# Two transformer layers on one core: the first norm of layer 1 transposed by DMA in two 16-bit planes

## The chip, the core and the metric

The kernel runs on one core of a Trainium2 chip. A core has a matrix engine (TensorE, PE in the profile, with its weight loads as PEld), a vector engine (VectorE, DVE), an engine for activation functions (ScalarE, ACT), a general engine (GpSimd, POOL), and SyncE (SP), which here issues DMAs only. They run side by side, each through its own list of instructions in order, and wait for one another through semaphores. The metric is the device time of one execution in microseconds (us); lower is better.

## What is computed

Inputs x (2 x 2048 tokens, 512 features) and a context of 2 x 128 tokens go through two layers. Each layer is an attention from x to the context and a feed-forward part, each with a layer norm in front and a residual sum behind:

```
x = x + L0_xattn(norm(x), context)      16 heads of 64, rotary positions, tanh cap
x = x + L0_ffn(norm(x))                 fake-quantised gate, up and down projections, 1408 wide
x = x + L1_xattn(norm(x), context)      16 heads of 32, with biases and a mask
x = x + L1_ffn(norm(x))                 a gate of 512 logits; the token's argmax modulo 8
                                        picks one of 8 experts (512 x 512)
norm(x) = (x - mean(x)) / sqrt(var(x) + 1e-5)
```

The change concerns the third line: the norm in front of layer 1's attention and the way its result reaches the query projection, Q = norm(x) Wq^T + bq. A matrix product on TensorE sums over the partitions, so the normed tile, whose partitions are tokens, has to be turned until its partitions are features.

## The kernel before

The 4096 tokens are 32 tiles of 128 tokens, one token per partition, and stay on the chip from end to end (`xs[n]`, 128 x 512 fp32). The kernel has four stretches: layer 0's attention (to about 680 us), the gate and up projections (to about 845 us), the down projection merged with the start of layer 1 (to about 950 us), and layer 1's attention merged with the gate of the experts and then the experts themselves (to the end).

The order of work is written out by hand. From the down projection on, TensorE, VectorE, ScalarE and GpSimd execute their instructions in exactly the order in which the program states them. Only SyncE's list, the DMAs, is put in order by the scheduler, and it too is then executed in order.

*The down projection* (loop at the end of the program, `for n in range(NT - held)`): for each tile n, `rounded(n + 2)` loads 704 KB of hidden values from memory and ScalarE rounds them to 8 bits (L798), `widened(n + 1)` makes bf16 of them on VectorE (L803), `down(n)` runs 11 matmuls on TensorE (L809), VectorE scales the result into `y` (two buffers, L811) and GpSimd adds it to x (L812). Near its end the first two pairs of tiles of layer 1 are prepared: their norms at n = 22 and 26, their turning (`turned1`) after the `down` of n = 23 and 27. In between, `queries` of block 0 run.

*The loop over tiles* (`for n in range(NT)`) has one tile per iteration and two tiles per block (`B1 = 256` tokens). The steps of iteration n that matter here, in program order:

- `biased(n - 1)`: GpSimd adds the output bias to the residual (L926).
- `rest1 = normed(...)`: the statistics of tile n + 4, which is tile t of block blk + 2: bn_stats on VectorE, then the power -1/2 on GpSimd (L100).
- `scores(n)`: 16 products of queries and keys on TensorE (L869), mask and maxima on VectorE.
- `queries(blk + 1, ...)`: half of this tile's share of the next block's query projection (L849), which reads `xT` of block blk + 1; ScalarE adds the bias (L852).
- `exponentials(n)` on ScalarE (L891); `shares(n, 0)`, `shares(n, 1)`: sums on VectorE, the products on GpSimd (L900); `logits(n - 2)` on TensorE (L955) between them.
- `rest1()`: VectorE centres and scales tile n + 4 into `xn1` (L820).
- `projected(n - 1)`, `normed2(n - 1)()`: the output projection (L932), then the second norm of that tile, again with a power on GpSimd and a centring on VectorE.
- the other half of `queries`; additions to the expert weights on GpSimd for tiles 4 to 19 (L1230); `turned(n)`: the shares transposed on TensorE and copied by ScalarE (L908); the store of a finished row tile to memory (L982); `turned2(n - 1)`: the second norm transposed, with a ScalarE copy (L949); `mixed(n)`: shares times values on TensorE (L918), copied by ScalarE to `oT` (L923).
- at the end of the block's second tile, `turned1` for both tiles of block blk + 2: four 128 x 128 transposes per tile on TensorE (L115) into PSUM, and a ScalarE copy into `xT` (L840). `xT` has one buffer; the next iteration's `queries` is its first reader, straight after `scores`.

During iterations 0 to 2 the eight expert weights of 1 MB each are loaded by SyncE.

Of the kernel before, what the change touches and what calls it, by code (L numbers as in the profile page):

```python
# [13 lines left out]
I32 = mybir.dt.int32  # L14
U32 = mybir.dt.uint32
U8 = mybir.dt.uint8
I8 = mybir.dt.int8
AF = mybir.ActivationFunctionType
ALU = mybir.AluOpType
# [4 lines left out]
P = 128  # L24
B, S, T, D = 2, 2048, 128, 512
ND = D // P
NT = B * S // P
# [31 lines left out]
NB1 = B1 // P  # L59
# [3 lines left out]
def two_layers(ctx: ExitStack, tc: tile.TileContext, a, out):  # L63
    nc = tc.nc
# [8 lines left out]
    def load(dst, src):  # L73
        nc.sync.dma_start(out=dst, in_=src)
# [36 lines left out]
    def transposed(psum, src, n=ND):  # L111

        pt = psum.tile([P, n, P], F32, name="pt", tag="m")
        for c in range(n):
            nc.tensor.transpose(pt[:, c, :], src[:, c * P : (c + 1) * P], ident)  # L115
        return pt
# [33 lines left out]
    with ExitStack() as l0:  # L150
        w0 = l0.enter_context(tc.tile_pool(name="w0", bufs=1))
        psm = l0.enter_context(tc.tile_pool(name="psm", bufs=2, space=PSUM))
# [13 lines left out]
        mid = l0.enter_context(tc.tile_pool(name="mid", bufs=2))  # L166
# [5 lines left out]
        cosk, sink = (xs[homes[22]][:, i * T : (i + 1) * T] for i in range(2))  # L172
        padu = w0.tile([P, B], U8, name="padu")
        for b in range(B):
# [152 lines left out]
        def normed(k):  # L327


            stats[k] = small.tile([P, NB0, 2], F32, name="stat")  # L330
            for t, n in enumerate(tiles[k]):
                mv = variance(xs[n])
                ve = small.tile([P, 1], F32, name="ve")
                nc.vector.tensor_scalar(ve, mv[:, 1:2], 1.0 + EPS, EPS * EPS, ALU.mult, ALU.add)
                nc.vector.tensor_copy(stats[k][:, t, 0:1], mv[:, 0:1])
                nc.gpsimd.tensor_tensor(stats[k][:, t, 1:2], ve, minus_half, ALU.pow)
            if k > 1:
                features_in(k)
                turned_in(k)
# [247 lines left out]
    bob = wa.tile([P, D], F32, name="bob")  # L587
    masks = wa.tile([P, TPB, T], U8, name="masks")
    ones1 = wa.tile([P, DH1], F32, name="ones1")


    def table(shape, pattern, base=0, channel=0, dtype=BF16):
# [17 lines left out]
        out=before, in_=before, pattern=[[1, P]], compare_op=ALU.is_ge, fill=0.0, base=-1, channel_multiplier=-1  # L610
# [25 lines left out]
    with ExitStack() as up:  # L636
        psm = up.enter_context(tc.tile_pool(name="psm_ff", bufs=2, space=PSUM))
# [99 lines left out]
        for blk in range(NT // NBF):  # L737
            for i in range(NI):
                pg = psg.tile([P, BF], F32, name="pg")
                pu = psg.tile([P, BF], F32, name="pu")  # L740
                for w, dst in ((wgT, pg), (wuT, pu)):
# [7 lines left out]
                h = work.tile([P, NBF, P], F32, name="h", bufs=4)  # L749
# [5 lines left out]
                    out=h_dram[blk * NBF : (blk + 1) * NBF, :, i, :].rearrange("t p q -> p t q"), in_=h  # L755
                )

                t, odd = divmod(i, 2)
                n = (blk + 1) * NBF + t
# [3 lines left out]
                if i >= 3 and i % 2 == 1:  # L763
                    n = (blk + 1) * NBF + (i - 3) // 2
# [9 lines left out]
        rest = values(0)  # L774
        sh, ish = act_step(psm, "L0_ffn_clip_down", hmax)
        rest()
        rest = values(1)
# [5 lines left out]
    psm = l1.enter_context(tc.tile_pool(name="psm_l1", bufs=4, space=PSUM))  # L783
    pss = l1.enter_context(tc.tile_pool(name="pss_l1", bufs=1, space=PSUM))
    big = at.enter_context(tc.tile_pool(name="big1", bufs=1))
    mid = at.enter_context(tc.tile_pool(name="mid1", bufs=2))
# [28 lines left out]
    scs, xTs, qTs, keeps, ss_, sums, pTs_, os_ = {}, {}, {}, {}, {}, {}, {}, {}  # L815
    xn1s = {}

    def center_by(dst, x, mean, r):

        nc.vector.scalar_tensor_tensor(dst, x, mean, r.to_broadcast([P, D]), ALU.subtract, ALU.mult)  # L820

    def normed(n):

        mv = variance(xs[n])
        r = small.tile([P, 1], F32, name="r")
        rsqrt_eps(r, mv[:, 1:2])

        def rest():
            xn1s[n] = mid.tile([P, D], F32, name="xn1")
            center_by(xn1s[n], xs[n], mv[:, 0:1], r)  # L830

        return rest

    def turned1(n):

        blk, t = divmod(n, NB1)
        if t == 0:
            xTs[blk] = big.tile([P, ND, B1], F32, name="xT1")
        pt = transposed(psm, xn1s[n])
        nc.scalar.copy(xTs[blk][:, :, t * P : (t + 1) * P], pt)  # L840

    def queries(blk, fs):

# [93 lines left out]
    def normed2(n):  # L937

        mv = variance(xs[n])
        nc.vector.tensor_copy(xw[n][:, D : D + 1], mv[:, 0:1])  # L940
        r = xw[n][:, D + 1 : D + 2]
        rsqrt_eps(r, mv[:, 1:2])
        xn2[n] = mid.tile([P, D], F32, name="xn2", bufs=1)
        return lambda: center_by(xn2[n], xs[n], mv[:, 0:1], r)
# [19 lines left out]
    def gated(n):  # L964

        negm, i8 = picks[n]
        pe = small.tile([P, 1], F32, name="pe1")

        nc.scalar.activation(
            scs[min(n + 2, NT - 1)][:, 0].rearrange("p c k -> p (c k)"), pls[n], AF.Exp, bias=negm, accum_out=pe  # L970
        )
        ei = small.tile([P, 1], U32, name="ei")
        nc.vector.tensor_scalar(ei, i8[:, 0:1], NE - 1, None, ALU.bitwise_and)
        ef = small.tile([P, 1], F32, name="ef")
        nc.vector.tensor_copy(ef, ei)
        nc.vector.tensor_scalar(hot[:, n, :], iota_e, ef, None, ALU.is_equal)
        nc.gpsimd.tensor_tensor(cum[:, n + 1, :], cum[:, n, :], hot[:, n, :], ALU.add)
        nc.vector.memset(xw[n][:, D + 3 : D + 4], 0.0)

        def rest():  # L980
            nc.vector.reciprocal(xw[n][:, D + 2 : D + 3], pe)
            nc.sync.dma_start(out=x_dram[n * P : (n + 1) * P, :], in_=xw[n])  # L982

        return rest
# [173 lines left out]
    held = 4  # L1158
    widened(0)
    rounded(1)  # L1160
    rests = []
    for n in range(NT - held):
        rounded(n + 2)
        widened(n + 1)
        for rest in rests:
            rest()
        down(n)
        rests = []
        if n == NT - held - 6:
            rests = [normed(t) for t in range(NB1)]  # L1170
        if n == NT - held - 5:
            for t in range(NB1):
                turned1(t)
        if n >= NT - held - 4:
            f = n - NT + held + 4
            queries(0, range(f, f + 1))
        if n == NT - held - 2:
            rests = [normed(NB1 + t) for t in range(NB1)]
        if n == NT - held - 1:
            for t in range(NB1):  # L1180
                turned1(NB1 + t)
# [5 lines left out]
    for n in range(NT):  # L1187
        blk, t = n // NB1, n % NB1
        ahead = blk + 1 < nblk
        fs = range(t * ND // NB1, (t + 1) * ND // NB1)  # L1190
        if n > 0:
            biased(n - 1)
        rest1 = normed((blk + 2) * NB1 + t) if blk + 2 < nblk else None
        scores(n)
        if ahead:
            queries(blk + 1, fs[:1])
        exponentials(n)
        if n == 0:
            for i in range(NT - held, NT - held + 2):
                down(i)  # L1200
                widened(i + 2)
        shares(n, 0)
        if n > 1:
            logits(n - 2)
        shares(n, 1)
        if rest1:
            rest1()
        if n > 0:
            projected(n - 1)
            normed2(n - 1)()  # L1210
        rest = gated(n - 2) if n > 1 else None
        if n + 1 < NT:
            kept_keys(n + 1)
        if ahead:
            queries(blk + 1, fs[1:])
        if n == 0:
            for i in range(NT - held + 2, NT):
                down(i)
            dwn.close()
            ffd.close()  # L1220
            moe = ctx.enter_context(tc.tile_pool(name="moe", bufs=1, side="right"))
            we = moe.tile([P, NE, ND, D], F32, name="we")
            for e in range(NE):
                load(we[:, e], a["L1_ffn_We"][e].rearrange("(c p) f -> p c f", p=P))
        if 4 <= n < 4 + 2 * NE:
            e, half = divmod(n - 4, 2)
            if half == 0:
                load(rowadd, v_dram[e].partition_broadcast(P))
            for c in range(2 * half, 2 * half + 2):
                nc.gpsimd.tensor_tensor(we[:, e, c, :], we[:, e, c, :], rowadd, ALU.add)  # L1230
        if not ahead:

            expert(n - NT + NB1)
        turned(n)
        if rest:
            rest()
        if n > 0:
            turned2(n - 1)
        mixed(n)
        if t == NB1 - 1 and blk + 2 < nblk:  # L1240
            for t in range(NB1):
                turned1((blk + 2) * NB1 + t)
        if n == NTA + 2:
            route = routing(True)
        if route:
            for _ in range(3 if n == NTA + 2 else 2):
                if next(route, route) is route:
                    route = None
                    for j in range(4):
                        gathered(j)  # L1250
                    break
        if n == NT - NB1 - 1:
            for j in range(2):
                centered_x(j)
            turned_x2(0)
# [57 lines left out]
```

## Time and profile before

| | us |
|---|---|
| median of 3 runs | 1624.31 (1623.14 to 1624.88) |
| the profiled execution's own time | 1623.87 |
| its span, first to last instruction | 1622.2 |
| TensorE busy | 1566.2 (97%) |
| VectorE busy | 1160.9 (72%) |
| ScalarE busy | 694.1 (43%) |
| GpSimd busy | 583.6 (36%) |
| copies of `turned1` on ScalarE (L840), 32 | 17.3, 0.589 each |
| centring of `xn1` (L820), 32 | 26.1, 0.821 each |

How to read it: a group line gives line, engine, operation, what is written from what, the shape and how often; then the busy time in total and the mean of one in ns; then how long the engine was idle just before these instructions, and what ended that. A timeline line gives the start, the length, and then the same names; a bracket at its end tells an idle time and its releaser. SPq is SyncE's queue: its times are those of issuing a DMA, not of moving the data. PEclk is the share of its clock that TensorE was granted. In the steady part of the loop, from about 975 us, two iterations take 31.8 us.

### The profile page before, as it was taken

Reading aid. Unit: us, or ns where it says so; the run is one execution under the profiler, and the core shown is the slowest. Engines: PE = TensorE matmul, PEld = TensorE weight load, DVE = VectorE, ACT = ScalarE, POOL = GpSimd, SP = SyncE. Lnnn points to the kernel's source line nnn. Section 1 sums busy time; section 2 is a strip of 40 time slices with the busy share of each in tenths; the row PEclk is TensorE's granted clock in tenths of the full one; section 3 lists DMA queues with packets and bytes.
Section 4 is the critical chain, followed back from the end, with each engine's and each line's share of the span. In section 5 each row is a group of like instructions: output and inputs, shape, how many; then the busy total and the mean of one; then the engine's idle time right before and its main releaser. Section 6 shows DMA issues by size and latency. Waiting matters only on the chain. (4 is left out here: it accounts for less than half of the span.)

```text
span 1622.2 us, 26285 instructions
## 1 busy us (share of the span) xinstructions
PE 1566.2 (97%) x9690; PEld 922.2 (57%) x9714; DVE 1160.9 (72%) x2276; ACT 694.1 (43%) x1537; POOL 583.6 (36%) x576
## 2 busy tenths in 40 slices
PE   7999999999999999999999989999999998999997
PEld 5655555655555565434444556666666665654443
DVE  3467777777777875689986678787787879766322
ACT  1222222222222222234336567676766765753332
POOL 2232222222222221110006644555656443544553
PEclk9999999999999999999999999999999999999999
DMA  9511112111111310567659650000000000113332
GB/s 323 178 37 40 46 41 55 40 46 40 47 46 36 77 37 5 160 174 189 180 168 314 221 202 20 28 21 34 27 21 27 14 21 14 40 47 108 128 121 68
DMA packets 135164, 139.64 MB, mean 86 GB/s; under 512 B 51681, under 2 KB 99257, under 8 KB 135036
## 3 DMA queue, kind: packets, MB, share of 16 engines
q1 hardware_dynamic: 125932, 118.07, 23.9%
q0 software_dynamic: 6240, 18.70, 3.6%
q8 instruction: 78, 1.28, 0.3%
q10 hardware_dynamic: 2864, 1.19, 0.3%
q14 instruction: 50, 0.41, 0.1%
HBM read 89.97 MB, written 41.79 MB: 81 GB/s over the span
## 5 line engine op out<-in xcount | busy, mean ns | idle before, releaser
L392 PE MATMUL pq<-xnT,wq 128*128 128x256 f32 x1024 | 254.4, 391 | 0.0
L418 ACT ACTIVATE pr<-sc 128x1024 f32<-128x1024 f32 x64 | 65.6, 1025 | 421.6 <-PE sc L413 421.5
L450 PE MATMUL pw<-wo,att 128*128 128x512 f32 x512 | 230.8, 593 | 0.0
L392 PEld LDWEIGHTS pq<-xnT,wq 128*128 128x128 f32 x1024 | 184.4, 189 | 67.1 <-issue 44.0
L900 POOL TENSOR_TENSOR s<-s,rs 128x1024 f32<-128x1024 f32 x64 | 132.6, 2085 | 185.1 <-DVE rs L899 184.7
L891 ACT ACTIVATE s<-s,mx 128x128 f32<-128x128 f32 x512 | 175.3, 388 | 20.8 <-DVE mx L882 20.8
L402 POOL TENSOR_TENSOR q<-rt,rt 128x256 f32<-128x256 f32 x64 | 46.8, 731 | 339.8 <-DVE rt L401 335.4
L450 PEld LDWEIGHTS pw<-wo,att 128*128 128x128 f32 x512 | 96.9, 190 | 96.4 <-issue 89.9
L440 DVE RECIPROCAL rd<-sc 128x256 f32<-128x256 f32 x64 | 112.4, 1757 | 46.6 <-PE sc L434 46.4
L1146 PE MATMUL pz<-we,x 128*128 x312 | 140.7, 594 | 0.7 <-issue 0.6
L849 PE MATMUL pq<-xT,wq 128*128 128x256 f32 x512 | 124.1, 385 | 0.1
L877 DVE SCALAR_TENSOR_TENSOR s<-sc,keep 128x1024 f32<-128x1024 f32 x64 | 78.0, 1219 | 53.5 <-PE sc L869 45.4
L932 PE MATMUL pw<-wo,oT 128*128 128x512 f32 x256 | 115.2, 592 | 0.7 <-ACT oT L923 0.7
L955 PE MATMUL pl<-wgate,xnT 128*128 128x512 f32 x256 | 115.3, 593 | 0.0
L849 PEld LDWEIGHTS pq<-xT,wq 128*128 128x128 f32 x512 | 94.8, 190 | 28.1 <-issue 13.9
L748 ACT ACTIVATE gate<-pg,gsc 128x512 f32<-128x512 f32 x88 | 60.5, 687 | 96.6 <-PE pg L743 81.4
L397 DVE TENSOR_TENSOR rt<-pq,rope_cos 128x256 f32<-128x256 f32 x64 | 27.0, 422 | 104.3 <-PE pq L392 104.3
L743 PE MATMUL pu<-xqT,wuT 128*128 128x512 bf16 x345 | 90.4, 382 | 4.2 <-DVE h L751 3.8
L91 DVE BATCH_NORM_STATS2 st<-x 128x6 f32<-128x512 f32 x130 | 89.4, 688 | 5.7 <-DMA x<-in_ctx 3.5
L1150 DVE TENSOR_TENSOR x<-x,x 128x512 f32<-128x512 f32 x39 | 27.0, 693 | 90.0 <-ACT x L1149 89.8
L743 PE MATMUL pg<-xqT,wgT 128*128 128x512 bf16 x344 | 90.1, 382 | 0.4
L1146 PEld LDWEIGHTS pz<-we,x 128*128 128x128 f32 x312 | 56.3, 190 | 58.3 <-issue 58.0
(216 smaller groups left out, 2791.9 us busy)
## 6 DMA issues: line engine op xcount, KB each, us to landing
h_dram<-h SPq DMA_DIRECT2D x88, 256.0 KB
hq<-h_dram SPq DMA_DIRECT2D x31, 704.0 KB
x_dram<-x SPq DMA_DIRECT2D x32, 258.0 KB
x<-in_x SPq DMA_DIRECT2D x32, 256.0 KB
we<-in_L_ffn_We SPq DMA_DIRECT2D x8, 1024.0 KB
xnT<-in_x_turned SPq DMA_DIRECT2D x14, 512.0 KB
along<-stat_dram SPq DMA_DIRECT2D x14, 256.0 KB
w_in<-in_L_ffn_w_gate SPq DMA_DIRECT2D x11, 256.0 KB
```

The lines of the kernel that those rows point to most:

```text
L91: nc.vector.bn_stats(out=st, in_=x)
L392: nc.tensor.matmul(pq, wqs[c // 2][:, c % 2, par, g * P : (g + 1) * P], xnTs[k][:, c, :], start=(c == 0), stop=(c == ND - 1))
L440: nc.vector.reciprocal(rd, sc[:, 0, B0:])
L450: nc.tensor.matmul(pw, atts[u][:, f, t * P : (t + 1) * P], wo[:, 2 * g + f, :], start=(g == 0 and f == 0), stop=(g == NG - 1 and f == 1),)
L743: nc.tensor.matmul(dst, w[:, c, i * P : (i + 1) * P], xqTs[blk][:, c, :], start=(c == 0), stop=(c == ND - 1),)
L849: nc.tensor.matmul(pq, wq1[:, c, f * P : (f + 1) * P], xTs[blk][:, c, :], start=(c == 0), stop=(c == ND - 1))
L877: nc.vector.scalar_tensor_tensor(s, sc[:, 2 * half : 2 * half + 2].rearrange("p r c k -> p (r c) k"), -MASKED, keeps[n].unsqueeze(1).to_br ...
L891: nc.scalar.activation(s[:, h, :], s[:, h, :], AF.Exp, bias=mx[:, h : h + 1], **accum)
L900: nc.gpsimd.tensor_tensor(s, s, rs.unsqueeze(2).to_broadcast([P, 8, T]), ALU.mult)
L932: nc.tensor.matmul(pw, os_[n][:, c, :], wo1[:, c, :], start=(c == 0), stop=(c == ND - 1))
L955: nc.tensor.matmul(pl, xn2T[n][:, c, :], wgate[:, c, :], start=(c == 0), stop=(c == ND - 1))
L1146: nc.tensor.matmul(pz, ring[j][:, c, :], we[:, bass.ds(e, 1), c, :], start=(c == 0), stop=(c == ND - 1))
```

## The change

`turned1` no longer uses TensorE. The centred tile `xn1` (128 tokens x 512 fp32) is regarded as 1024 numbers of 16 bits. GpSimd copies them into a tile `planes`, all 512 low halves first and then all 512 high halves (`split`). A transposing DMA, issued by SyncE, turns the eight blocks of 128 x 128 16-bit numbers and writes them back into `xn1`. ScalarE then copies the two planes into `xT` so that the halves of each fp32 lie side by side again (`joined`): 1024 16-bit elements per partition, read in a row and written at steps of four bytes.

In the loop over tiles, `split` stands after `projected(n - 1)` and `normed2(n - 1)`; `joined` stands where the ScalarE copy was. In the down projection `split` follows the centring directly, and the norms of the first two pairs are moved earlier: from n = 22 to 19 and from n = 26 to 23. The turning of both pairs stays where it was.

```diff
+    def split(x):
+        planes = mid.tile([P, 2 * D], U16, name="planes")
+        nc.gpsimd.tensor_copy(
+            planes.rearrange("p (h f) -> p h f", h=2), x.bitcast(U16).rearrange("p (f h) -> p h f", h=2)
+        )
+        nc.sync.dma_start(
+            out=x.bitcast(U16).rearrange("p (b q) -> p b q", q=P), in_=planes, transpose=True
+        )
+
+    def joined(dst, x):
+        nc.scalar.copy(
+            dst.bitcast(U16).rearrange("p c (q h) -> p h c q", h=2),
+            x.bitcast(U16).rearrange("p (h c q) -> p h c q", h=2, c=ND),
+        )
...
             center_by(xn1s[n], xs[n], mv[:, 0:1], r)
+            return lambda: split(xn1s[n])
...
-        pt = transposed(psm, xn1s[n])
-        nc.scalar.copy(xTs[blk][:, :, t * P : (t + 1) * P], pt)
+        joined(xTs[blk][:, :, t * P : (t + 1) * P], xn1s[n])
...
         for rest in rests:
-            rest()
+            rest()()
         down(n)
         rests = []
-        if n == NT - held - 6:
+        if n == NT - held - 9:
             rests = [normed(t) for t in range(NB1)]
         if n == NT - held - 5:
             for t in range(NB1):
                 turned1(t)
+            rests = [normed(NB1 + t) for t in range(NB1)]
...
-        if n == NT - held - 2:
-            rests = [normed(NB1 + t) for t in range(NB1)]
...
         if rest1:
-            rest1()
+            rest1 = rest1()
         if n > 0:
             projected(n - 1)
             normed2(n - 1)()
+        if rest1:
+            rest1()
```

More of the change, by code (lines that the diff above doesn't have):

```diff
@@ L16 @@
 U8 = mybir.dt.uint8
+U16 = mybir.dt.uint16
 I8 = mybir.dt.int8
```

## The prediction

> **What bounds the kernel now.** I read the busy shares first, then the stretch in which the changed step runs, then that stretch's timeline instruction by instruction.
>
> ```profile
> PE 1566.2 (97%) x9690; PEld 922.2 (57%) x9714; DVE 1160.9 (72%) x2276; ACT 694.1 (43%) x1537; POOL 583.6 (36%) x576
> ```
> ```profile
> 975.00:1300.00 325.00, 317.84 (x2432) 213.81 (x2431) 257.75 (x555) 226.25 (x724) 178.07 (x155) 1.00 0.07 23
> ```
>
> In the window table (columns: length, then busy time of PE, PEld, DVE, ACT, POOL, then clock, DMA share, GB/s) TensorE is busy for 318 of 325 us while ScalarE and GpSimd have slack. So taking TensorE work away pays, if nothing that TensorE then waits for comes later than the work taken away. The timeline at the end of an odd tile decides that:
>
> ```profile
> 1124.22 0.55 POOL L100 TENSOR_TENSOR x<-ve,minus_half 128x1 f32<-128x1 f32 x1
> ...
> 1126.26 1.08 PE L918 MATMUL po<-s,v 128*32 128x128 f32 x32
> ...
> 1127.27 1.09 PE L115 MATMUL pt<-ident,xn 128*128 128x128 f32 x8
> 1127.43 0.59 ACT L923 COPY oT<-po 128x512 f32<-128x512 f32 x1 [0.38 <-PE po L918]
> 1127.96 1.07 ACT L840 COPY xT<-pt 128x512 f32<-128x512 f32 x2
> ...
> 1128.29 1.17 PE L869 MATMUL sc<-kT,qT 32*128 32x128 f32 x32
> ...
> 1129.40 1.99 PE L849 MATMUL pq<-xT,wq 128*128 128x256 f32 x8
> ```
>
> The eight transposes occupy TensorE from 1127.27 to 1128.29: 1.02 us. The scores take to 1129.40, and then the next queries read xT, whose two copies ended at 1129.03, 0.37 us early. This is a relay with little room: whatever makes xT ready later than about 1128.4 (1129.40 less the 1.02 saved) stops TensorE, since its order is fixed.
>
> **The change part by part.** Sixteen groups of eight transposes go: two before the loop over tiles, fourteen in it (ends of tiles 1, 3, ... 27). TensorE's order is otherwise as before, so the change does take that work away.
>
> *A block of the loop.* In GpSimd's program order the new copy stands behind the small power instruction shown above (it ends at 1124.77), and its input, the centred tile, is ready since 1122.3. Its price C is not in the trace; nearest rows:
>
> ```profile
> L900 POOL TENSOR_TENSOR s<-s,rs 128x1024 f32<-128x1024 f32 x64 | 132.6, 2085 | 185.1 <-DVE rs L899 184.7
> L349 POOL TENSOR_TENSOR xnT<-xnT,along 128x1024 f32<-128x1024 f32 x14 | 34.9, 2493 | 0.0
> L422 POOL TENSOR_SCALAR_AFFINE_SELECT pr<-pr 128x512 f32<-128x512 f32 x8 | 5.1, 638 | 17.6 <-issue 15.4 <-ACT pr L420 1.5 <-POOL rstd L100 0.7
> L418 ACT ACTIVATE pr<-sc 128x1024 f32<-128x1024 f32 x64 | 65.6, 1025 | 421.6 <-PE sc L413 421.5
> L840 ACT COPY xT<-pt 128x512 f32<-128x512 f32 x32 | 17.3, 589 | 3.9 <-PE pt L115 3.8
> ```
>
> Between 0.64 us (the one-input row, if size cost nothing) and 2.49 us (two inputs of 1024). The copy has one input like L422 and twice its elements: C = 2 x 0.638 = 1.28. It ends at 1126.1. Behind it on GpSimd stand the additions to the expert weights (2.5 us), the bias and a power; these end at 1130.6 now, and the next shares start at 1135.3, so 4.7 us of slack hides C.
>
> SyncE then issues the DMA (0.1 us for the semaphore). It stands ahead of the row store of tile n-2, which nothing waits for until the gathers of the end; SyncE is idle for most of the 15.4 us of a tile. The landing time T comes from two quiet transposes of 512 and 1408 rows of 256 bytes:
>
> ```profile
> 515.92 1.20 SPq L297 DMA_TRANSPOSE wuT<-wb  x1
> ...
> 595.45 1.41 SPq L310 DMA_TRANSPOSE wdT<-wb  x1
> ```
> ```profile
> 517.05:517.90 0.85, 0.85 (x20) 0.51 (x17) 0.76 (x2) 0.27 (x1) 0.00 (x0) 1.00 0.78 154
> ...
> 597.50:598.50 1.00, 1.00 (x7) 0.87 (x6) 1.00 (x1) 0.00 (x0) 0.00 (x0) 1.00 1.01 184
> 598.50:599.00 0.50, 0.50 (x3) 0.26 (x2) 0.47 (x2) 0.00 (x0) 0.00 (x0) 1.00 0.00 0
> ```
>
> Their data moves until about 2.0 and 3.0 us after the issue began, and their completion is recorded at 2.42 and 3.51. For 1024 rows the line between gives T = 2.42 + 1.09 x 512/896 = 3.04, ends 2.42 and 3.51. Landed: 1124.83 + 1.28 + 0.1 + 3.04 = 1129.25.
>
> The Trainium skill, "VectorE: DVE Perf Modes", section on the three transpose paths, speaks against the change: it gives a 128x128 bf16 block 390 ns on TensorE and 1309 ns on the DMA crossbar. Eight blocks one after another would be an estimated 10.5 us, a wait of some 9.5 us per block, and a total near 1750. The trace has four blocks complete in 2.42 us and eleven in 3.51, so the blocks of one DMA overlap; I go by the rows.
>
> ScalarE's join has 1024 elements where the copy had 512: J between 0.59 (same bytes as L840) and 1.47 (the 1408-element activation of L798), taken as 1.03 from L418. The first join follows oT at 1128.0 and ends at 1129.05; the second waits for the DMA, 1129.25 to 1130.28. TensorE resumes at 1130.4. Its scores now end at 1127.27 + 1.10 = 1128.37: it waits 2.03 us for the 1.02 saved, **+1.01 per block**. The exponentials queued behind the joins move with the queries, and the shares still end about 0.3 us before TensorE wants them, as now (1124.10 against 1124.37). Thirteen such blocks: **+13.1**.
>
> *The clock.* The wait may also cost clock:
>
> ```profile
> 910.30:913.71 3.41, 1.46 (x10) 1.00 (x10) 3.34 (x8) 0.59 (x1) 1.58 (x3) 1.00 0.94 363
> 913.71:917.13 3.42, 3.42 (x9) 1.22 (x8) 0.67 (x1) 1.96 (x2) 1.80 (x1) 0.50 0.21 67
> ...
> 958.08:961.50 3.42, 1.71 (x12) 1.24 (x10) 1.72 (x5) 2.55 (x14) 2.84 (x2) 1.00 1.04 391
> ```
>
> TensorE idle for 1.95 us inside one 3.41 us window was followed by a window at clock 0.50; idle 1.71 us was not. Half clock for 3.41 us loses 1.7 us. A 2.03 us wait lies at least 1.85 us within one window in (3.41 - 2.03 + 0.36)/3.41 = 51% of positions, so six blocks of thirteen: **+10.2** (ends 0 and 13 x 1.7 = 22).
> The Trainium skill, "TensorE: Matmul & The Clock Gate", rules for kernel authors, says to avoid gaps over about 3 us; by it 2 us gaps would be free and the sum 10 us lower. The 1.95 us gap above says otherwise.
>
> *Tile 1.* Its transposing DMA follows eight 1 MB loads of the expert weights in SyncE's queue:
>
> ```profile
> 950.22 13.10 SPq L74 DMA_DIRECT2D we<-in_L_ffn_We  x8
> ```
> ```profile
> 963.30:975.85 12.55, 11.11 (x100) 7.70 (x99) 7.73 (x10) 6.44 (x16) 2.01 (x3) 0.86 0.89 330
> 975.85:976.50 0.65, 0.65 (x3) 0.26 (x2) 0.65 (x1) 0.65 (x5) 0.00 (x0) 1.00 0.00 0
> ```
>
> Those land at 975.85. GpSimd's copy is done near 964.8, but the queue's data is in order, so the planes land near 977.5 and the second join ends at 978.5. TensorE wants xT at 969.44: it waits 9.2 us for 1.02 saved, +8.2, and a half-clock window after it, +1.7: **+9.9**. If the DMA overtook the loads this would be about +1; both ends are kept.
>
> *Before the loop.* First pair: now TensorE idles 1.95 us for the centred tile, transposes for 1.15 and pays a half-clock window (4.8 us in all); queries start at 917.59. After the change the planes stand behind about 1 MB of loads that land at 911.1, arrive near 914, and two joins end near 916: **-1.5** (ends -4.8 and +1). GpSimd's two copies delay its additions by 2.6 us, which the two y buffers of VectorE just absorb. Second pair: 1.0 saved, but ScalarE is busy without a gap from 931.8 to 943.6 and two joins add 1.0 there: **0**, ends -1 and +1. Its DMAs are issued four tiles ahead and hidden by that.
>
> VectorE's work is unchanged.
>
> **Sum.** 13.1 + 10.2 + 9.9 - 1.5 + 0 = +31.7 us. The profiled execution took 1623.87 (span 1622.2, 1.7 around it), so 1655.6; the median of the runs is 0.44 higher: **1656 us**.
>
> **Rivals.**
> - *Relay just kept* (C, T and J near their low ends): landed 1128.0, joins end at 1129.2, wait 0.93, net -0.1 per block, no clock loss; the tile 1 wait remains: 13 x -0.1 + 9.9 - 1.5 = +7, 1631. For it: the same bytes as before go through ScalarE. Against: every ScalarE row of the trace goes by elements.
> - *Slow pieces* (C 2.49, T 3.51, J 1.47): landed 1130.9, wait 4.1, net +3.1 per block (40), a clock window each (22), 9.9 - 1.5: +71, 1695. Against: strides of four bytes in the 16-bit views would have to cost both engines.
> - *Tile 1 not delayed*: the DMA overtakes the loads: 8.9 less, 1647.
> - *All hidden* (the other side): both joins end before 1128.4, so TensorE keeps its 1.02 in thirteen blocks and 1.0 in the second pair: -14.3 - 1.5 + 9.9 = -5.9, 1618. The break-even point is a wait of 1.02, joins ended by 1129.3; faster needs less. Against: oT alone ends at 1128.0 in ScalarE's fixed order, and two joins after it cannot end before 1128.4 at any row's price.
>
> **How the numbers follow.** The sum as worked 0.70, tile 1 not delayed 0.08, relay just kept 0.09, slow pieces 0.10, all hidden 0.03. A change of 0.2% (3 us) is about what this kernel's runs can tell. Slower 0.96, same 0.01, faster 0.03. The range runs from a little over the relay case to most of the way to the slow pieces: 1635 to 1687.
>
> **What would show it.** Right: in the changed profile TensorE's queries (now L867) wait about 2 us at every second tile on ScalarE's join; some 3.4 us windows in the loop at clock 0.5; a 9 us TensorE gap near 970; a join of about 1.03 us and a GpSimd copy of about 1.3 us. Wrong: no wait ahead of the queries (all hidden), joins over 1.5 us or GpSimd copies over 2 us (slow pieces), no clock loss after 2 us waits (10 us less).

## The result, and the profile after

The changed kernel takes 1672.55 us (median; 1669.3 to 1673.96), 1.0294 times the kernel before, 95% interval 1.0279 to 1.0309. Predicted were 1656, in a range of 1635 to 1687. Its profiled execution took 1673.03 us with a span of 1671.3, 49.1 more than before. One of the five executions of a version tried below (p_lead) took 3237.26 us, twice the others; nothing here gives a cause, and the ratio leaves it out. The busy shares of the page show what kind of loss it is:

```profile
PE 1555.7 (93%) x9563; PEld 911.6 (55%) x9586; DVE 1185.0 (71%) x2276; ACT 715.6 (43%) x1537; POOL 615.0 (37%) x608
```

TensorE works 10.5 us less than before, as the change promises, and waits 60 us more. ScalarE and GpSimd have more to do, as foreseen. VectorE has 24 us more, although the change gives it no instruction. To place the loss, I compare the start of each tile's scores in the two traces and take the difference stretch by stretch:

| stretch | predicted, us | measured, us |
|---|---|---|
| up to the scores of tile 0 (first pair, down stage, and the second pair's eight transposes) | -1.5 | -2.05 |
| iteration 0 (queries of the second pair) | 0 | +3.60 |
| iterations 1 and 2 (the "tile 1" term) | +9.9 | +11.80 (-2.59, then +14.39) |
| tiles 3 to 31, thirteen blocks | +13.1 and +10.2 clock = +23.3 | +34.71 |
| after that | 0 | +1.04 |
| sum | +31.7 | +49.1 |

Most of what the forecast lacks lies in the thirteen blocks. The timeline of the changed kernel at the end of an odd tile answers to the one in the prediction (start, length, engine, line, what is written from what; the bracket is idle time and who ended it):

```profile
1147.31 0.55 POOL L101 TENSOR_TENSOR x<-ve,minus_half 128x1 f32<-128x1 f32 x1
1147.81 1.04 POOL L827 COPY planes<-xn 128x1024 uint16<-128x1024 uint16 x1
1147.90 1.50 DVE L821 SCALAR_TENSOR_TENSOR xn<-x,mv 128x512 f32<-128x512 f32 x1 [0.66 <-POOL x L101]
1148.88 1.23 SPq L830 DMA_TRANSPOSE xn<-planes  x1
...
1149.54 0.63 PE L116 MATMUL pt<-ident,xn 128*128 128x128 f32 x4 [1.20 <-DVE ei L991]
...
1151.11 1.17 PE L887 MATMUL sc<-kT,qT 32*128 32x128 f32 x32
1151.27 0.59 ACT L941 COPY oT<-po 128x512 f32<-128x512 f32 x1 [0.38 <-PE po L936]
1151.75 2.54 ACT L835 COPY xT<-xn 128x1024 uint16<-128x1024 uint16 x2
...
1154.35 1.99 PE L867 MATMUL pq<-xT,wq 128*128 128x256 f32 x8 [2.06 <-ACT xT L835]
```

The last line is the forecast wait: 2.06 us for xT, predicted 2.03. The two joins run without a pause, 2.54 us together (1.27 a piece), and end it; the DMA, issued at 1148.88 and recorded as landed 3.05 us later, is in time for the second join (1153.0). The surprise is in the third line. The centring of the *second* norm takes 1.50 us where it took 0.75, beside GpSimd's new copy, and the transposes of xn2 behind it wait 1.20 us instead of 0.36 (the bracket names `ei`, the instruction that VectorE runs next, but it is the centred tile that they read). In the kernel before, the two lines were:

```profile
1124.80 0.75 DVE L820 SCALAR_TENSOR_TENSOR xn<-x,mv 128x512 f32<-128x512 f32 x1 [0.66 <-POOL x L100]
...
1125.70 0.63 PE L115 MATMUL pt<-ident,xn 128*128 128x128 f32 x4 [0.36 <-ACT s L908]
```

The tile shown is one of three odd tiles of the thirteen blocks with 1.20; nine have 1.11, and the even tiles 0.75. So a steady block costs 2.06 - 1.02 + (1.11 - 0.36) + (0.75 - 0.36) = 2.18 us. The starts of the scores say nearly the same: +2.54 and -0.27 for its two tiles in most blocks, 2.27 together. The groups give the means over the whole run (busy us, mean ns, idle before and its releasers):

```profile
L867 PE MATMUL pq<-xT,wq 128*128 128x256 f32 x512 | 129.0, 396 | 44.9 <-ACT xT L835 44.9
L821 DVE SCALAR_TENSOR_TENSOR xn<-x,mv 128x512 f32<-128x512 f32 x32 | 44.3, 1383 | 21.6 <-POOL x L101 21.6
L835 ACT COPY xT<-xn 128x1024 uint16<-128x1024 uint16 x32 | 41.4, 1337 | 14.9 <-DMA xn<-planes 13.5 <-DVE s L895 1.4
L827 POOL COPY planes<-xn 128x1024 uint16<-128x1024 uint16 x32 | 35.2, 1104 | 0.7 <-DVE xn L821 0.7
```

The second centring's mean was 783 ns before and is 1383 now.

In the iteration after the expert-weight loads the wait is longer. The lines are of the same timeline, then of a table by windows (length, then busy time of PE, PEld, DVE, ACT, POOL, then clock, DMA share, GB/s):

```profile
966.09 8.54 SPq L830 DMA_TRANSPOSE xn<-planes  x1
...
979.57 1.33 ACT L835 COPY xT<-xn 128x1024 uint16<-128x1024 uint16 x1 [9.27 <-DMA xn<-planes]
...
980.95 2.50 PE L867 MATMUL pq<-xT,wq 128*128 128x256 f32 x5 [11.45 <-ACT xT L835]
```
```profile
972.30:975.70 3.40, 0.00 (x0) 0.00 (x0) 2.17 (x2) 0.00 (x0) 0.00 (x0) 0.50 1.04 386
...
982.50:986.00 3.50, 3.50 (x8) 2.25 (x7) 0.00 (x0) 1.23 (x4) 0.00 (x0) 0.50 0.00 0
```

TensorE waits 11.45 us, the clock is at 0.50 from 972.3 to 986.0, and the 5 us that TensorE works in that time lose half, 2.5 us.

### The profile page after: what moved, and what is told of

It reads as the page before. It is cut to its first block, busy times and chain, and to the rows that moved or that the text cites. A ratio compares the mean times of both kernels' runs of the same rounds, so it can differ in the third digit from the quotient of the medians.

```text
span 1671.3 us, 26185 instructions
## 1 busy us (share of the span) xinstructions
PE 1555.7 (93%) x9563; PEld 911.6 (55%) x9586; DVE 1185.0 (71%) x2276; ACT 715.6 (43%) x1537; POOL 615.0 (37%) x608
## 5 line engine op out<-in xcount | busy, mean ns | idle before, releaser
L419 ACT ACTIVATE pr<-sc 128x1024 f32<-128x1024 f32 x64 | 65.5, 1024 | 421.5 <-PE sc L414 421.4
L867 PE MATMUL pq<-xT,wq 128*128 128x256 f32 x512 | 129.0, 396 | 44.9 <-ACT xT L835 44.9
```

The costliest lines, as they stand in the source:

```text
L867: nc.tensor.matmul(pq, wq1[:, c, f * P : (f + 1) * P], xTs[blk][:, c, :], start=(c == 0), stop=(c == ND - 1))
```

## The experiments

### The copy alone, in 16 and in 32 bits

The kernel before, plus GpSimd's copy; nothing reads it.

```diff
+    def split(x):
+        planes = mid.tile([P, 2 * D], U16, name="planes")
+        nc.gpsimd.tensor_copy(
+            planes.rearrange("p (h f) -> p h f", h=2), x.bitcast(U16).rearrange("p (f h) -> p h f", h=2)
+        )
...
             normed2(n - 1)()
+        if rest1:
+            split(xn1s[(blk + 2) * NB1 + t])
```

In the second kernel the copy is `nc.gpsimd.tensor_copy(planes.bitcast(F32), x)`.

> The kernel before, with GpSimd's 16-bit copy of each tile's normed rows added in the loop where the change has it; nobody reads the planes, there is no DMA transpose and no join, and TensorE still transposes. Theory (while GpSimd copies 16-bit words, VectorE's centring of the second norm stands still): that centring goes from 0.75 to about 1.50 us, TensorE's transposes of xn2 wait about 1.2 us in odd tiles and 0.75 in even ones instead of 0.36, so about +1.1 us a block of two tiles, 14 blocks, +13 to +16 us: about 1638. Rival (what is lost in the loop comes from the joins and the DMA alone): the copy is hidden in GpSimd's idle time, 1622 to 1627.

> As the run before, but GpSimd copies the same 2 KB of each partition as 512 contiguous fp32 words, not as 1024 16-bit words in two planes; nobody reads the copy. Theory A (any GpSimd copy beside the centring holds VectorE up): the centring is near 1.2 to 1.5 us and the time is 8 to 15 us above the kernel before, in proportion to the copy's length. Theory B (only the 16-bit copy does it, since VectorE's 0.83 us beside GpSimd's 4.2 us fp32 multiplications is no longer than elsewhere): the centring stays at 0.75 to 0.85 and the time at 1622 to 1627.

Measured: 1641.17 us with the 16-bit copy, ratio 1.0114 (1.0094 to 1.0134), somewhat more than expected, since the transposes of xn2 wait 1.10 us here in even tiles too, and 1629.44 us with the 32-bit copy, ratio 1.0043 (1.003 to 1.0055). The timeline of the first, then of the second:

```profile
1111.46 1.04 POOL L825 COPY planes<-xn 128x1024 uint16<-128x1024 uint16 x1
1111.54 1.50 DVE L821 SCALAR_TENSOR_TENSOR xn<-x,mv 128x512 f32<-128x512 f32 x1 [0.66 <-POOL x L101]
...
1113.19 0.63 PE L116 MATMUL pt<-ident,xn 128*128 128x128 f32 x4 [1.10 <-DVE ei L980]
```
```profile
1109.36 0.61 POOL L825 COPY planes<-xn 128x512 f32<-128x512 f32 x1
1109.44 1.07 DVE L821 SCALAR_TENSOR_TENSOR xn<-x,mv 128x512 f32<-128x512 f32 x1 [0.66 <-POOL x L101]
...
1110.66 0.63 PE L116 MATMUL pt<-ident,xn 128*128 128x128 f32 x4 [0.68 <-DVE ei L980]
```

Without DMA or join, the copy alone costs TensorE 0.74 us a tile. It is the copy's presence and not its word size: in both kernels the centring ends 0.54 us after the copy does (1113.04 after 1112.50; 1110.51 after 1109.97), as if VectorE stood still until GpSimd is through and then needed 0.54. My theory B, that only 16-bit words do this, is refuted; theory A's price, 8 to 15 us, was above the 6.1 measured: the copy takes only 0.61 us and leaves 0.32 us a tile.

The trace of the kernel before had this row, in the only tile where the second norm's centring falls beside another GpSimd instruction, and the prediction passed over it:

```profile
963.49 1.27 POOL L926 TENSOR_TENSOR x<-x,bob 128x512 f32<-128x512 f32 x1
963.56 1.75 DVE L820 SCALAR_TENSOR_TENSOR xn<-x,mv 128x512 f32<-128x512 f32 x1 [0.66 <-POOL x L100]
```

1.75 us instead of 0.75, ending at 965.31, again 0.55 after GpSimd.

### The centring with one tensor input

```diff
-        return lambda: center_by(xn2[n], xs[n], mv[:, 0:1], r)
+        return lambda: center(xn2[n], xs[n], mv[:, 0:1], r)
```

`center` is a `tensor_scalar` of x with the mean and 1/sigma as per-partition scalars; `center_by` reads 1/sigma as a broadcast second tensor.

> The changed kernel with one instruction in another form: the second norm's centring reads only x as a tensor and takes the mean and 1/sigma as per-partition scalars (a tensor_scalar, as in layer 0), where it read 1/sigma as a second, broadcast tensor. What stops VectorE is disputed. Theory A (a VectorE instruction with two tensor inputs in SBUF waits until GpSimd's instruction ends; in the rows so far the centring ends 0.54 to 0.55 us after whatever GpSimd instruction it overlaps): with one input it takes 0.55 to 0.75 us beside the copy, the transposes of xn2 wait 0.36 us or less in both tiles, the wait for xT stays near 2 us, and 13 blocks save 1.2 us each: 1653 to 1660. Theory B (GpSimd's 16-bit copy stops any VectorE instruction): the centring still ends 0.5 us after the copy, 1668 to 1674.

Measured: 1673.15 us, ratio 1.0311 (1.0281 to 1.034): no gain.

```profile
1110.26 1.04 POOL L827 COPY planes<-xn 128x1024 uint16<-128x1024 uint16 x1
1110.34 1.23 DVE L104 TENSOR_SCALAR xn<-x,mv 128x512 f32<-128x512 f32 x1 [0.66 <-POOL x L101]
```

Theory A falls: the one-input form is held up too. Where nothing runs beside it, it takes 0.55 us; here it ends 0.28 us after the copy. Theory B's "any VectorE instruction" is too wide, though. In the same trace batch statistics (0.70 us), maxima out of SBUF (1.22) and additions with an operand in PSUM (0.69) last as long beside GpSimd's multiplications and additions as without, and the down projection's scaling, which also reads PSUM, keeps its 0.69 us beside the 16-bit copy itself. Why the 0.27 us that this form gains in each tile don't show in the time: the blocks are 0.55 us shorter, but eight half-clock windows fall into the thirteen blocks here and three in the changed kernel, at 1.7 us each.

The Trainium skill, "SBUF — State Buffer", section "Who interferes with whom", states that VectorE and GpSimd share one pair of SBUF ports under an exclusive lock. By it, a VectorE instruction with two inputs in SBUF contends with a GpSimd instruction that reads SBUF, and so does VectorE in a mode that uses both its ports (which a `tensor_scalar` can enter); the second one to issue is blocked until the first finishes. The rows here agree for both forms of the centring. They do not show the ports themselves.

### The joins ahead of the copy of the mixed heads

```diff
-        mixed(n)
         if t == NB1 - 1 and blk + 2 < nblk:
             for t in range(NB1):
                 turned1((blk + 2) * NB1 + t)
+        mixed(n)
```

> The changed kernel, with the two joins put ahead of the copy of the mixed heads (oT) in ScalarE's order. Theory (in the steady block the wait for xT lasts until ScalarE, which starts late, is through two joins of 1.27 us; the DMA has landed by then): the joins start about 0.85 us earlier (0.37 us of idle time and 0.48 of the oT copy's pitch), the wait falls from 2.06 to about 1.2 us, 13 blocks: 9 to 13 us less than the changed kernel, about 1661. Rival (the landing of the second tile's DMA sets the end of the wait): the second join waits for it and the time falls by 3 us or less, 1669 to 1673.

Measured: 1660.78 us, ratio 1.0239 (1.0217 to 1.0262), 11.8 below the changed kernel.

```profile
1144.20 2.55 ACT L835 COPY xT<-xn 128x1024 uint16<-128x1024 uint16 x2
...
1146.62 0.57 ACT L941 COPY oT<-po 128x512 f32<-128x512 f32 x1
1146.80 1.99 PE L867 MATMUL pq<-xT,wq 128*128 128x256 f32 x8 [1.11 <-ACT xT L835]
```

The wait falls from 2.06 to 1.11, as expected. So in the steady block the wait is ScalarE's two joins and their place in its order, not the DMA, which had landed at 1145.33, 0.1 us before the second join began. In four of the thirteen blocks the wait stays at 2.6 to 2.95 us. There the second tile's DMA takes 4.56 to 4.89 us to land instead of 3.05, and the rival is right: the landing sets the end of the wait.

### The split after the centring

```diff
-        if rest1:
-            rest1()
         rest = gated(n - 2) if n > 1 else None
+        if rest1:
+            rest1()
```

> The changed kernel with one thing moved: GpSimd's copy and the DMA come after the running counts, so after VectorE's centring of the second norm. Theory (two costs that trade: the centring beside the copy, 0.84 us of odd and 0.39 of even tiles, and the wait for xT, which ends with the landing plus a join): the centring is back at 0.75 and the transposes of xn2 wait 0.36 in both tiles, but the DMA starts about 1.7 us later, lands after the first join, and TensorE waits 3.3 to 3.8 us for xT instead of 2.06; a block is 0 to 0.8 us dearer than in the changed kernel, and the longer waits bring a half-clock window of 1.7 us to most blocks: 1675 to 1700. Rival (the standstill is the whole loss of the loop and the wait for xT doesn't move): 1.2 us less in each of 13 blocks, about 1657.

Measured: 1709.28 us, ratio 1.0528 (1.0507 to 1.0549): dearer than expected.

```profile
1122.53 0.63 PE L116 MATMUL pt<-ident,xn 128*128 128x128 f32 x4 [0.35 <-DVE ei L991]
1123.19 1.04 POOL L827 COPY planes<-xn 128x1024 uint16<-128x1024 uint16 x1
...
1127.49 1.33 ACT L835 COPY xT<-xn 128x1024 uint16<-128x1024 uint16 x1 [1.33 <-DMA xn<-planes]
...
1128.87 3.78 PE L867 MATMUL pq<-xT,wq 128*128 128x256 f32 x8 [3.48 <-ACT xT L835]
```
```profile
1124.60:1128.00 3.40, 0.80 (x31) 0.60 (x24) 2.42 (x3) 2.07 (x3) 3.40 (x4) 1.00 0.48 98
1128.00:1131.40 3.40, 2.53 (x6) 2.08 (x7) 2.37 (x3) 0.82 (x1) 0.41 (x1) 0.50 0.27 70
1131.40:1134.80 3.40, 3.40 (x6) 1.79 (x6) 0.00 (x0) 2.11 (x7) 0.00 (x0) 0.50 0.00 0
```

The trade is as the theory had it: the transposes of xn2 wait 0.35 again, and the wait for xT ends with the landing plus one join. It is 3.48 us in the block shown, but above the expected 3.8 in seven of the thirteen (4.03 on average). What I had too low besides is the clock: it stays at 0.50 for 6.8 us, not 3.4, in twelve of the thirteen blocks. Why it takes a second window here is not shown.

### The expert weights later

```diff
-            for e in range(NE):
-                load(we[:, e], a["L1_ffn_We"][e].rearrange("(c p) f -> p c f", p=P))
+        if 2 <= n < 2 + NE:
+            load(we[:, n - 2], a["L1_ffn_We"][n - 2].rearrange("(c p) f -> p c f", p=P))
```

> The changed kernel, with the eight 1 MB loads of expert weights issued one an iteration from iteration 2 on instead of all in iteration 0. Theory (tile 5's transposing DMA waits in the queue behind these loads): the wait of 11.45 us for xT at the end of iteration 1 falls to 2 to 3 us and the 13.7 us of half clock there go, so 10 to 13 us less than the changed kernel: about 1661. Rival (the wait there is the first in the loop and comes from something else, or the loads do the same damage wherever they stand): no less than 1669.

Measured: 1667.08 us, ratio 1.0285 (1.0253 to 1.0318).

```profile
950.13 7.97 SPq L75 DMA_DIRECT2D we<-in_L_ffn_We  x6
```
```profile
971.72 1.33 ACT L835 COPY xT<-xn 128x1024 uint16<-128x1024 uint16 x1 [4.03 <-DMA xn<-planes]
...
973.10 3.64 PE L867 MATMUL pq<-xT,wq 128*128 128x256 f32 x8 [6.21 <-ACT xT L835]
```

SyncE's order is not written by hand, and six of the loads still went out ahead of iteration 1's transposing DMA. The wait fell from 11.45 to 6.21 us: half an answer. So the loads were given to ScalarE, whose order is fixed:

```diff
+        if 2 <= n < 2 + NE:
+            nc.scalar.dma_start(out=we[:, n - 2], in_=a["L1_ffn_We"][n - 2].rearrange("(c p) f -> p c f", p=P))
```

> The changed kernel, with the eight 1 MB loads of expert weights issued by ScalarE, one an iteration, from the end of iteration 2 on; so they are behind no transposing DMA of their queue in time. Theory (tile 5's DMA lands 13 us late because the loads stand before it, as e_we_late showed in part: six of its loads were still issued ahead, the landing took 8.16 us and the wait 6.21): the landing takes 3 to 3.5 us, the wait at the end of iteration 1 is 2 to 3 us, the step there is 2.5 to 4 us instead of 14.4, and the time 1659 to 1664. Rival (the first transposing DMA of the loop is slow by itself, or the loads slow the later ones as much): 1667 or more.

Measured: 1667.05 us, ratio 1.0261 (1.0238 to 1.0284).

```profile
963.69 1.23 SPq L830 DMA_TRANSPOSE xn<-planes  x1
968.43 1.33 ACT L835 COPY xT<-xn 128x1024 uint16<-128x1024 uint16 x1 [0.52 <-DMA xn<-planes]
969.81 2.50 PE L867 MATMUL pq<-xT,wq 128*128 128x256 f32 x5 [2.71 <-ACT xT L835]
```

The mechanism is confirmed in the trace: the DMA lands after 4.66 us instead of 13.40 (3 to 3.5 were expected), the wait is 2.71, and the step that was 14.39 is 4.86. But the time fell by 5.5 us only, to where the rival had it. Of the 9.5 saved at this step, 4.6 are given back in the thirteen blocks, where seven half-clock windows fall into the trace instead of three. One of them follows an ordinary wait of 2.07 us:

```profile
1106.39:1109.80 3.41, 1.52 (x48) 1.13 (x40) 2.03 (x4) 3.03 (x4) 3.41 (x4) 1.00 0.66 175
1109.80:1113.21 3.41, 3.23 (x8) 2.60 (x9) 3.08 (x3) 0.13 (x1) 0.31 (x1) 0.50 0.93 326
```

### The relay one tile ahead

If the two losses of the block are matters of place, a version that moves copy and join out of the way must gain the removed transposes. (Not among the lines shown: the additions to the expert weights move behind the copy in GpSimd's order.)

```diff
-        planes = mid.tile([P, 2 * D], U16, name="planes")
+        planes = mid.tile([P, D], F32, name="xn2", bufs=1).bitcast(U16)
...
-            xTs[blk] = big.tile([P, ND, B1], F32, name="xT1")
+            xTs[blk] = big.tile([P, ND, B1], F32, name="xT1", bufs=2)
...
-        rest1 = normed((blk + 2) * NB1 + t) if blk + 2 < nblk else None
+        rest1 = normed(n + 5) if n + 5 < NT else None
...
             turned2(n - 1)
+        if rest1:
+            rest1()
...
+    normed(2 * NB1)()()
     kept_keys(0)
...
-        if t == NB1 - 1 and blk + 2 < nblk:
-            for t in range(NB1):
-                turned1((blk + 2) * NB1 + t)
+        if n + 4 < NT:
+            turned1(n + 4)
```

> A version of the changed kernel with the relay one tile ahead and off the waits: iteration n centres and splits tile n+5 instead of n+4 and joins tile n+4 at its end, so that each DMA has a whole iteration to land; GpSimd copies after the running counts, when VectorE's centring of the second norm is done, into the buffer that this norm leaves free; xT has two buffers. Theory (the loss of the change is the wait for the second join and the VectorE standstill, both matters of place): no wait for xT in the loop, the transposes of xn2 wait 0.36 us again, and the 1.02 us of transposes a block are really saved: 14 blocks, 14 us below the kernel before, 1606 to 1613. Rival (GpSimd's copy stops VectorE wherever it stands, and something on the path waits for VectorE; or the join delays ScalarE's queries): at least +0.7 us a tile somewhere, 1618 to 1640.

Measured: 1640.1 us, ratio 1.0102 (1.0083 to 1.012). Expected were 1606 to 1613.

```profile
1112.59 1.34 ACT L835 COPY xT<-xn 128x1024 uint16<-128x1024 uint16 x1
...
1113.98 1.99 PE L867 MATMUL pq<-xT,wq 128*128 128x256 f32 x8 [0.87 <-ACT xT L835]
```

My plan had a hole: the join of an odd tile, at the end of the iteration, is read by the very next queries. It cost 0.87 us of the 1.02 in each of the thirteen blocks; the loop otherwise behaved, with 0.25 to 0.36 us ahead of the xn2 transposes. The start was worse: iteration 1's planes lay in the second norm's buffer while their DMA waited behind the weight loads (a step of 11.62 us). Mended:

```diff
+        if n + 4 < NT:
+            turned1(n + 4)
         if ahead:
             queries(blk + 1, fs[1:])
...
-        if n + 4 < NT:
-            turned1(n + 4)
+        if 2 <= n < 2 + NE:
+            nc.scalar.dma_start(out=we[:, n - 2], in_=a["L1_ffn_We"][n - 2].rearrange("(c p) f -> p c f", p=P))
```

> p_lead with three places mended that its trace shows. The join of tile n+4 stands before the second half of the queries in ScalarE's order, in the 1.6 to 2.0 us in which ScalarE waits for TensorE there, instead of at the iteration's end, where TensorE waited 0.87 us for it in every second tile; the expert weights are loaded by ScalarE, one an iteration from iteration 2 on, instead of all eight ahead of tile 6's transposing DMA (a step of 11.6 us); and the planes of the down stage's pairs take turns in two buffers. Theory (all that is left then is the removed 1.02 us of transposes a block): the steady block is 1.0 us shorter than in the kernel before, 14 blocks, and the start of the loop within 3 us of it: 1606 to 1614. Rival (the join, 1.34 us in a gap of 1.6, holds back the queries' copies and with them the copies of the turned shares, for which TensorE waits): the block is no shorter than before, 1620 to 1632.

> The kernel before, with only the expert weights loaded as in p_lead2, by ScalarE, one an iteration from iteration 2 on. Theory (nothing in the kernel before stands behind these loads in its queue until the first rows of x are written in iteration 2): no change, 1621 to 1627, so that what p_lead2 gains is the relay's. Rival (the eight loads at once also hold up the kernel before, or their issue on ScalarE costs time): 1617 or less, or 1630 or more.

Measured: p_lead2 takes 1609.86 us, ratio to the kernel before 0.9917 (0.9903 to 0.993). The control, the kernel before with only the loads moved, takes 1621.22, ratio 0.999 (0.9981 to 0.9999), within 0.2%. So of the 13.5 us that p_lead2 gains on the kernel before, 11.4 remain against the control.

```profile
1115.31 1.89 PE L867 MATMUL pq<-xT,wq 128*128 128x256 f32 x8
...
1115.55 1.34 ACT L835 COPY xT<-xn 128x1024 uint16<-128x1024 uint16 x1
...
1118.41 0.75 DVE L821 SCALAR_TENSOR_TENSOR xn<-x,mv 128x512 f32<-128x512 f32 x1 [0.66 <-POOL x L101]
1119.31 0.63 PE L116 MATMUL pt<-ident,xn 128*128 128x128 f32 x4 [0.36 <-ACT s L926]
...
1120.06 1.04 POOL L827 COPY xn<-xn 128x1024 uint16<-128x1024 uint16 x1
1120.88 1.17 PE L887 MATMUL sc<-kT,qT 32*128 32x128 f32 x32
...
1121.98 1.99 PE L867 MATMUL pq<-xT,wq 128*128 128x256 f32 x8
```

The join fits where ScalarE waits for TensorE's queries, the centring is back at 0.75, the copy comes 0.9 us after it, and the queries follow the scores without a wait. By the starts of the scores a steady block takes 30.73 us instead of 31.75, 1.02 less, which is what the removed transposes took.

## Why the prediction was right, and which steps were not

The direction, the range and the chief mechanism held: TensorE's order is fixed, and what replaced 1.02 us of its work came 2.06 us later. That the total also lies in the range is in part the range's width: it reached up to the slow pieces, and 14 us of the loss come from a cost that no term of the sum held.

- *The relay's wait, +1.01 a block.* Measured +1.04 (2.06 for 1.02) in eight of the thirteen blocks. That it agrees so closely is luck, since its terms erred and cancelled: C 1.28 against 1.04 measured, T 3.04 against 3.05, J 1.03 against 1.27. With C and T as measured the planes land before the second join can begin, so the joins' length sets the wait, and not the landing as I had it; e_join_first shows it. In the other five blocks the wait is 2.24 to 2.98 us: there the second tile's DMA took 4.58 to 4.89 us to land, and the landing does set it. That adds 3.3 us.
- *"VectorE's work is unchanged."* This is the step that failed, by 14 us: over the thirteen blocks the transposes of xn2 wait 23.5 us, where they waited 9.4. The work was unchanged, its duration was not. I had looked for what was queued behind the copy on GpSimd and on SyncE, and not for what ran beside it. e_copy16 shows it alone, 17.9 us above the kernel before.
- *The clock, +10.2.* Three half-clock windows in the thirteen blocks instead of six. TensorE works 9.5 us in them, so they cost 4.7. The rule used (1.95 us idle in a 3.41 us window cuts, 1.71 does not) held, but the ordinary wait, which was to meet it in half of the blocks, never did in the changed kernel: none of the eight waits of 2.04 to 2.08 us was followed by half clock. Two of the three windows follow waits of 2.98 and 2.94 us, the third other waits in iteration 25. The 51% took all places of the wait in the window as equally likely. But a steady block of 34.02 us is only 0.11 us short of ten windows of 3.413, so the wait falls at nearly the same place block after block. Seven windows in e_we_act and eight in e_one_input show what another place does.
- *The blocks together.* For TensorE: 30.1 us of waits for xT, 14.1 more ahead of the transposes of xn2, 1.3 less ahead of those of the shares, and 8.2 less busy time (the removed transposes, less the half clock) make 34.7, as measured.
- *"Tile 1", +9.9.* Measured +11.80 over iterations 1 and 2: a wait of 11.45 instead of 9.2 (the planes landed at 979.49, not 977.5, since all transfers were some 2.5 us later; the join took 1.33), and 13.7 us of half clock instead of 3.4, of which 5 us were work. e_we_act confirms the queue as the cause.
- *Before the loop.* Of the -2.05 up to the scores of tile 0, about 1 us are the second pair's transposes, which stood ahead of them; so the first pair gave about -1 for -1.5. The second pair is wrong: 0 with ends of -1 and +1, measured about 3.6 - 1 = +2.6, a wait of 1.87 us for xT at 933.6 and a half-clock window at 934.8. It is the same relay as in the loop: ScalarE's joins run from 931.02 to 933.53, and TensorE wants xT from 931.7 on. A window of the kernel before, at 964.9, is gone in exchange; it is in the -2.59 of iteration 1.
- *The rivals.* Slow pieces (1695) had too high prices, but the 1709 of e_split_late shows how near that regime is: one step moved. All hidden (1618) was excluded for this order of ScalarE, and rightly; with another order, p_lead2, the cover exists and 1610 is reached.

## What to carry to other kernels

When work moves to an idle engine, look at what runs beside it in the new place as well as at what queues behind it; here a copy on GpSimd held up VectorE until it was through, and the trace of before had one overlap that showed it. A relay over three engines paid once its DMA had an iteration to land in and its join stood where ScalarE waits anyway: copy, DMA and join cost 49 us in one order and saved 11 to 13 in another. Loads that hurt nobody became a wait as soon as something urgent was put behind them in their queue.

## What the hardware showed

- VectorE's centring of 128 x 512 fp32 takes 0.75 us alone. Beside a GpSimd instruction on 512 or more elements that began first it ends 0.54 to 0.55 us after that instruction in nearly all cases: a 16-bit copy, a 32-bit copy, the bias addition, and also the first of the two multiplications of the shares, beside which the first norm's centring has always stood (0.82 us; it starts about 1.6 us into 1.9). The power on one element per partition does not hold it up. With one tensor input it takes 0.55 us alone and ends 0.28 us after the copy.
- The clock: counted in steps of 3.41 us from the half-clock stretches, every full-clock window of the traces (the loop, 940 to 1500 us) in which TensorE was idle for 1.90 us or more was followed by one at 0.50, and none with 1.70 or less; between 1.7 and 1.9 both occur. The Trainium skill, "TensorE: Matmul & The Clock Gate", section "Why this matters for your kernels", says to avoid gaps over about 3 us; the runs here put the limit lower, at 1.7 to 1.9 us of idle time within one window.
- A transposing DMA of 1024 rows of 256 bytes lands in 3.04 to 3.11 us in 17 of the changed kernel's 28 iterations and behind the expert weights in 13.40, but in 4.45 to 4.9 in ten (iterations 2 to 4, 13 to 16, 25 to 27), and at nearly the same places in the versions that issue it at the same point of the iteration. Five of these ten lengthen a wait for xT, and two of the three half-clock windows follow such waits. In the trace, each of the ten overlaps a packet of 16 KB of queue q8, which the profile lists as "instruction"; it starts 1.9 to 2.9 us after the issue, and 7 to 74 of the 1024 rows are moved only after 2.7 us, where all of a quick one's are through. But four of the 17 quick landings overlap such a packet as well. No run removed it, so whether it is the cause stays open.
- GpSimd's copy of 1024 16-bit words takes 1.04 us, of 512 fp32 words 0.61; ScalarE's join of 1024 16-bit words at steps of four bytes 1.33 alone, and 2.54 for two in a row.
